# Two attention blocks on a batch of eight: where a stage's weight sums, one job's statistics and one layer's output bias are made

## The chip, the core and the metric

The kernel runs on one core of a Trainium2 chip, in one launch. The metric is the time of one execution on the device in microseconds (us); less is better. All arithmetic is in float32.

## What is computed

The input x has 8 images of 512 channels and 32 x 32 positions. Two layers of the same kind are applied to each image. A layer normalises x over 8 groups of channels, makes q, k and v by products with 512 x 512 weights, runs attention with 8 heads of 64 channels over the 1024 positions, multiplies by an output weight and adds x. The second layer has the same form with weights of its own.

```python
xg = x.reshape(B, GROUPS, -1)
xn = ((xg - mean) * lax.rsqrt(var + EPS)).reshape(B, C, H, W) * gamma + beta
qkv = einsum('oc,bchw->bohw', qkv_w, xn) + qkv_b
attn = softmax(einsum('bhds,bhdt->bhst', q, k) * scale, axis=-1)
out = einsum('bhst,bhdt->bhds', attn, v).reshape(B, C, H, W)
return x + einsum('oc,bchw->bohw', proj_w, out) + proj_b
```

## The kernel before

A **job** is one image in one layer. There are 16, in the order (image 0, layer 0), (1, 0), (0, 1), (1, 1), (2, 0), (3, 0), (2, 1), ... (L103). The jobs are numbered from 0, so job 2 is the first of layer 1 and job 3 the fourth of all. For every job the kernel runs two sections, which follow each other on TensorE without overlap:

- **Stage n** makes what attention n needs and finishes what attention n-1 left: first v of job n (`v_phase`, L482), then in `deep_phases` (L574) the output product O of job n-1 and k and q of job n. In this text "stage 2" is the one with O of job 1 and k and q of job 2.
- **Attention n** (`Attention.run`, L984) has 64 steps: four score products (L870), ScalarE's exp (L875), VectorE's running sum of the exponentials (L885, L887), and four value products two steps later (L901). After every eight steps `finish` closes a group (L917 to L978). Chores, small jobs of the next stage, are hung on step numbers (slots).

**The products of a stage.** All four weights are multiplied by a seven-product scheme (Strassen's, in Winograd's form). For O, k and q it is nested: seven outer **chains**, and in each chain seven products of 128 x 128 by 256 columns. So `deep_phases` has 21 chains c = 0 to 20: 0 to 6 are O, 7 to 13 k, 14 to 20 q. The seven products of a chain run in the order 1, 5, 6, 2, 7, 3, 4 and two chains are interleaved (L762): the product at place j of chain c stands at 7c + 2j. ScalarE copies or adds a bias (L438, L442, L646, L648, L657). VectorE reads PSUM after product 7 and after product 3 (L653, L655, in `put`). Product 4 adds to the bank that VectorE has to read after product 7, so TensorE can't start product 4 before that read has ended.

**What VectorE does between the reads.** After product 7 and after product 3 of a chain there is a **slot** (L744): it takes one thing from the first of three queues that is not empty: `soon`, `outer`, `extra`. `soon` holds sums that the coming chains need. `outer` holds the additions that put the outer products together (L668), among them the additions of O's parts to x (L684). `extra` holds work of later sections, each with the chain before which it isn't taken: the statistics of the job after (L234), the loading of an output bias and its four sums (`make_out_bias`, L1065). What `extra` still holds at the end of the stage is put on the first slots of the attention that follows (L1298).

**Weight sums.** A chain needs seven 128 x 128 matrices: four come from DRAM, and three are their sums, made in place with four VectorE instructions (`prepare`, L194, through `factor`, L151). It is done the first time a weight is used, and the result is stored in DRAM for all later jobs. So layer 0's O is prepared in stage 1, layer 1's k and q (14 chains) in stage 2 and layer 1's O in stage 3. `begin(c)` (L586), which runs with the first product of chain c, prepares chain c + 2. VectorE's order is the program's, so those four instructions stand ahead of whatever VectorE instruction comes next, which is the read after product 7 of chain c - 1.

**Additions to x by DMA.** Some of O's parts are added to x not by VectorE but by an accumulating DMA that GpSimd issues (L682, in `more`, L674). In stage 2 there are four: parts 1 and 2 to the quarter (0, 0) of x, part 3 to the quarter (0, 1), part 4 to the quarter (1, 0). VectorE adds the other parts to the same quarters. The framework keeps accesses to the same bytes in the order in which the program issues them, by semaphores. Each outer product lies in a buffer of a pool of six (`epool`), which the exponentials of the attention use as well.

**Statistics.** `norm_steps(n)` (L355) gives the steps of job n's normalisation. Usual form: eight `bn_stats` on VectorE in `extra`, a gather over DRAM (L271), then in the attention before job n the group values (L281), the factors (L301) and four ScalarE passes that write the normalised x (L308). Job 1 has another form: in attention 0 ScalarE makes the sums and the sums of squares (`sums` L242, `squares` L251) in eight passes over x, whose main output goes to the buffer of the normalised x and is overwritten later. With that form the chores have later slots (L1301 to L1304), and the additions on the normalised x (L377 to L391 in `combine`) stand at slots 41, 44, 47, 50 and not at 36, 39, 42, 45.

The engines TensorE, VectorE and ScalarE run in the program's order (`manual_schedule`, L1544). The framework orders the queues of SyncE and GpSimd, so a load can be issued ahead of where the program has it, once its buffer is free.

Of the kernel before, what the change touches and what calls it, by code (L numbers as in the profile page):

```python
# [28 lines left out]
NT = S // P  # L29
HALF = S // 2  # L30
HP = NH // 2
NVEC = 6 * NC
GAMMA, BETA, BQ, BK, BP, BV = (i * NC for i in range(6))
SUM_LIMIT = 1e10
# [38 lines left out]
def fast_path(  # L73
# [281 lines left out]
    def norm_steps(n):  # L355
        norm = Norm(n)

        def place():
            xn[0] = acts.tile([P, NC, S], F32, tag="xn", name=f"xn_{n}")

        def factors():
            norm.factors(slice(0, NC))
            if n > 1:
                place()

        if n == 1:
            reads = [place] + [lambda cc=cc: norm.sums(cc) for cc in range(NC)]
            reads.append(norm.less_mean)
            reads += [lambda cc=cc: norm.squares(cc) for cc in range(NC)]
            reads.append(lambda: (norm.by_count(), norm.gather()))  # L370
            return reads, [norm.groups, factors] + [lambda cc=cc: norm.apply(cc) for cc in range(NC)]
        reads = [lambda cc=cc, sh=sh: norm.stat(cc, sh) for cc in range(NC) for sh in range(2)]
        reads.append(norm.gather)
        steps = [norm.groups, factors] + [lambda cc=cc: norm.apply(cc) for cc in range(NC)]
        return reads, steps
# [198 lines left out]
    def deep_phases(n, extra, outs=None, early=()):  # L574
# [8 lines left out]
        def job(which):  # L583
            return n - 1 if which == O else n

        def begin(c):  # L586
            which, o = chains[c]
            m = job(which)
            b, layer = jobs[m]
            if o == OUTER[0] and which != O:  # L590
                name = "k" if which == K else "q"
                dst[which] = acts.tile([P, NC, S], F32, tag=name, name=f"{name}_{n}")
                (kt if which == K else qt)[0] = dst[which]
            if c + 2 < len(chains):
                ahead, oo = chains[c + 2]
                prepare((job(ahead), ahead, oo))
            if which == O and c in (3, 4):
                soon.extend(outs.steps(c + 2))
            e = epool.tile([P, 2, HALF], F32, tag="e", name=f"p_{n}_{c}")
            tiles[which, o] = e  # L600
            s5 = small.tile([P, QT], F32, tag="s5", name=f"s5_{n}_{c}", bufs=3)
            half = (c + len(chains)) % 2
            ends = c + 1 == len(chains)
            names = "yvzu" if ends else ("vyuz", "zyuv")[(c // 2) % 2]
            z, y, u, w = (bank(half, b, f"{b}d_{n}_{c}")[:, :QT] for b in names)
            if which == O:
                r = right(outs.src, to[0], o)
                sums = outs.at[c]
            else:
                r = right(xn[0], tx[0], o)  # L610
                if o in (4, 5, 6):
                    d = deep_t[0][:, :, {5: 0, 6: 1, 4: 2}[o], :]
                else:
                    d = deep_x[0][:, :, {1: 0, 7: 1, 2: 2, 3: 3}[o], :]
                sums = [d[:, i, :] for i in range(4)]
            moving = {
                1: r[:, 0, :QT], 2: r[:, 1, :QT], 3: r[:, 1, QT:],
                5: sums[0], 6: sums[1], 7: sums[2], 4: sums[3],
            }
            lhs = held[m, which, o]  # L620

            def bias(oo):
                if o in (1, 6, 7):
                    return None
                oc = oo if o == 2 else 2 + oo
                if which == O:
                    return (
                        out_step[:, layer, oo : oo + 1] if o == 3
                        else out_bias[:, layer, oc : oc + 1]
                    )  # L630
                if o == 3:
                    return bias_step[:, layer, int(which == Q), oo : oo + 1]
                return env.vec(layer, BK if which == K else BQ, oc)

            def product(i, ps, start):
                nc.tensor.matmul(  # L636
                    ps, lhs[:, FACTOR[i], :], moving[i], start=start, stop=True,
                    skip_group_check=True,
                )

            def put(oo, ph, ps):
                to_ = e[:, oo, ph * QT : (ph + 1) * QT]
                b = bias(oo)
                if ph == 0:
                    if b is None:
                        nc.scalar.copy(to_, ps)  # L646
                    else:
                        nc.scalar.activation(to_, ps, AF.Identity, bias=b)  # L648
                elif ends and oo == 1:
                    nc.scalar.activation(to_, ps, AF.Identity, bias=b)  # L650
                    nc.vector.tensor_add(to_, to_, s5)
                elif b is None:
                    nc.vector.tensor_add(to_, ps, s5)  # L653
                else:
                    nc.vector.scalar_tensor_tensor(to_, ps, b, s5, ALU.add, ALU.add)  # L655

            return chain(product, lambda ps: nc.scalar.copy(s5, ps), put, z, y, u, w)  # L657
# [618 lines left out]
    for n in range(-1, len(jobs)):  # L1276
        last = n + 1 == len(jobs)
        outs = None
        if n >= 0:
            chores = {}  # L1280

            def put(i, fn):
                while i in chores:
                    i += 1
                chores[i] = fn

            if last:
                w = last_weights(n)
                for i, fn in enumerate(last_sums(0)):
                    put(44 + 3 * i, fn)  # L1290
            else:
                if n == 0:
                    first_factors(put, [(O, 0), (V, 1)])
                elif n == 1:
                    first_factors(put, [(K, 1), (Q, 1)])
                elif n == 2:
                    first_factors(put, [(O, 1)])
                for i, (_, fn) in enumerate(extra):  # L1298
                    put(2 + i, fn)
                at = (10, 19, 22, 24, 26, 28, 36, 39, 42, 45)  # L1300
                if n == 0:  # L1301
                    for i, fn in zip((3, 3, 4, 5, 6, 8, 10, 11, 12, 13, 15), reads):
                        put(i, fn)
                    at = (22, 30, 34, 35, 37, 38, 41, 44, 47, 50)  # L1304
                for i, fn in zip(at, steps + sums(n + 1)):
                    put(i, fn)
                deep_first = deep_steps(n + 1)
                for at, fn in zip((52, 54, 57, 59), deep_first[4:]):
                    put(at, fn)
                put(61, lambda: (extend_plan(n + 1), [fetch() for _ in range(RING)]))  # L1310
            assert max(chores, default=0) < NT * len(att.groups)
            att.run(chores)
            banks(0, "one")
            banks(1, "one")
            if last:
                for i, fn in enumerate(last_sums(1)):
                    later(4.1 + 1.5 * i, fn)
                later(9.9, judge)
                for sh in range(2):
                    last_proj(n, w, sh)  # L1320
                break
            outs = OutputSums(n)
            out_sums(n, outs)
            first = v_phase(n + 1, ORDER)
            for thunk in first[:-1]:
                thunk()
            rest = first[-1:]
            extra = deque()
            if jobs[n][1] == 1 and jobs[n][0] + 2 < B:
                extra.append((11, lambda b=jobs[n][0] + 2: (x_tile(b), load_x(b))))  # L1330
            if n == 1:
                load, bias_steps = make_out_bias(1)
                extra.append((8, load))
                extra.extend((11, fn) for fn in bias_steps)
            if n + 2 < len(jobs):
                reads, steps = norm_steps(n + 2)
                extra.extend((15, fn) for fn in reads)
        both = deep_phases(n + 1, extra, outs, deep_first[:4] if outs else ())
        both[0]()
        rest[0]()  # L1340
        if n < 0:
            later(22.0, lambda: load_x(1))
        for thunk in both[1:]:
            thunk()
        banks(0, "two")
        att = Attention(n + 1)
        att.scores(0)
        att.scores(1)
        banks(1, "two")
        att.scores(2, "po")  # L1350
# [249 lines left out]
```

## Time and profile before

| what | value |
|---|---|
| runs of the kernel before | 3206.60, 3208.58 and 3208.76 us, median 3208.58 us |
| the profiled execution's own time | 3205.31 us |
| span of its profile | 3203.5 us |
| TensorE busy | 3184.0 us, 99% |
| VectorE busy | 2773.0 us, 87% |
| ScalarE busy | 1913.1 us, 60% |
| GpSimd busy | 100.7 us, 3% |
| chain that ended last | TensorE 95%, VectorE 4% |
| bytes moved | 308.32 MB, 96 GB/s over the span |

The span runs from the first to the last instruction; 1.8 us of the execution's time lie around it. In the views below, a line names an instruction by its line in the kernel, its engine, its operation and what it writes and reads ("out<-in", buffer numbers left out). PE is TensorE's matmul, PEld its weight load, DVE VectorE, ACT ScalarE, POOL GpSimd. In a list of waits the engine and instruction that waited stand left of the arrow and the one that let it go right of it, with the total in us, the number of times and the longest. In a timeline each line has the start and the duration in us, and in brackets how long the engine was idle before it and who released it. Matmuls are pipelined and their ends are modelled, so a short wait of TensorE shows a little smaller than it is.

### The profile page before, as it was taken

What the parts mean: (1) busy time and instruction counts of PE and PEld (TensorE: products, weight loads), DVE (VectorE), ACT (ScalarE), POOL (GpSimd) and SP (SyncE); (2) the same over time, 40 slices, a digit from 0 to 9 for tenths busy, and PEclk for the clock granted to TensorE, in tenths of its full rate; (3) what the DMA queues carried; (4) which work ended last, traced back from release to release, by engine and by line L of the source; (5) the groups of instructions that cost most, each with busy time, mean ns of one, the idle gap of its engine ahead of it and who ended that gap; (6) DMA issues with size and microseconds to landing.
All of it is one profiled execution on the core that took longest, in us unless ns stands there. A gap on an engine that the chain in (4) does not pass through costs nothing.

```text
span 3203.5 us, 57787 instructions
## 1 busy us (share of the span) xinstructions
PE 3184.0 (99%) x22917; PEld 1861.8 (58%) x22917; DVE 2773.0 (87%) x3989; ACT 1913.1 (60%) x3063; POOL 100.7 (3%) x95
## 2 busy tenths in 40 slices
PE   9999999999999999999999999999999999999999
PEld 7366384663836648366483754837547375573844
DVE  8897999979889798897988889888898888988877
ACT  4746646466565665656656565565656656566564
POOL 0000000000000000000000000000000000000000
PEclk9999999999999999999999999999999999999999
DMA  8234172350703315033160421505216051150511
GB/s 291 74 108 126 49 215 69 94 167 22 213 25 91 88 28 159 21 105 130 30 210 16 119 67 38 147 16 142 96 44 194 16 141 44 51 135 20 170 37 42
DMA packets 156998, 308.32 MB, mean 96 GB/s; under 512 B 34104, under 2 KB 60592, under 8 KB 156464
## 3 DMA queue, kind: packets, MB, share of 16 engines
q1 hardware_dynamic: 139856, 272.05, 26.5%
q0 software_dynamic: 16864, 32.51, 6.2%
q8 instruction: 181, 2.97, 0.4%
q14 instruction: 97, 0.79, 0.1%
HBM read 225.13 MB, written 45.68 MB: 85 GB/s over the span
## 4 chain that ended last, share of the span: by engine, by line
PE 95%; DVE 4%; DMA 0%; issue 0%; POOL 0%; ACT 0%; DVEq 0%; POOLq 0%
PE sc L870 27%; PE po L901 27%; PE zd L636 10%; PE vd L636 10%; PE z L494 6%; PE yd L636 5%; PE ud L636 4%; PE y L494 2%; PE v L494 2%; PE u L494 2%; DVE acc L887 0%; DMA x<-p 0%; PE z_last L814 0%; DVE w L156 0%; DVE p L655 0%
## 5 line engine op out<-in xcount | busy, mean ns | idle before, releaser
L875 ACT ACTIVATE e<-sc 128x1024 f32<-128x1024 f32 x1024 | 1044.3, 1024 | 564.2 <-PE sc L870 458.7
L870 PE MATMUL sc<-q,k 64*64 64x512 f32 x8192 | 1058.2, 589 | 0.0
L901 PE MATMUL po<-e,v 64*64 64x512 f32 x8192 | 1057.3, 589 | 0.0
L887 DVE TENSOR_TENSOR acc<-acc,e 128x1024 f32<-128x1024 f32 x768 | 936.4, 1219 | 58.7 <-ACT e L875 12.0
L901 PEld LDWEIGHTS po<-e,v 64*64 64x64 f32 x8192 | 313.2, 133 | 565.7 <-issue 553.3
L870 PEld LDWEIGHTS sc<-q,k 64*64 64x64 f32 x8192 | 311.5, 133 | 562.4 <-issue 544.8
L885 DVE TENSOR_TENSOR acc<-e,e 128x1024 f32<-128x1024 f32 x128 | 156.4, 1222 | 112.2 <-ACT e L875 112.1
L636 PE MATMUL zd<-deep,w 128*128 128x256 f32 x860 | 241.1, 380 | 2.7 <-DVE p L653 2.1
L636 PE MATMUL vd<-deep,w 128*128 128x256 f32 x804 | 224.3, 380 | 1.4 <-DVE p L655 1.3
L636 PEld LDWEIGHTS zd<-deep,w 128*128 128x128 f32 x860 | 162.8, 190 | 27.2 <-DVE p L653 3.4
L636 PEld LDWEIGHTS vd<-deep,w 128*128 128x128 f32 x804 | 152.3, 190 | 23.9 <-DVE p L655 2.5
L917 DVE TRANSPOSE_TENSOR_REDUCE r<-acc 128x32 f32<-128x1024 f32 x128 | 158.5, 1238 | 0.6
L682 POOL DMA_DIRECT2D x<-p x62 | 74.6, 1211 | 1971.4 <-ACT p L646 1525.1
L636 PE MATMUL vd<-os,w 128*128 128x256 f32 x420 | 118.1, 380 | 1.6 <-DVE p L655 1.6
L668 DVE TENSOR_TENSOR p<-p,p 128x1024 f32<-128x1024 f32 x94 | 114.2, 1215 | 0.0
L494 PE MATMUL z<-w,t 128*128 128x256 f32 x480 | 110.9, 379 | 0.0
L494 PE MATMUL z<-w,xn 128*128 128x256 f32 x480 | 110.1, 382 | 0.0
L518 ACT COPY v<-z 128x512 f32<-128x512 f32 x32 | 18.7, 585 | 148.7 <-PE z L494 148.7
L494 PEld LDWEIGHTS z<-w,xn 128*128 128x128 f32 x480 | 90.0, 190 | 23.8 <-issue 12.2
L442 ACT COPY ud<-zd 128x256 f32<-128x256 f32 x156 | 55.7, 357 | 76.6 <-PE zd L636 75.7
L653 DVE TENSOR_TENSOR p<-vd,s 128x256 f32<-128x256 f32 x63 | 26.7, 424 | 85.1 <-PE vd L636 85.1
L657 ACT COPY s<-vd 128x256 f32<-128x256 f32 x156 | 58.0, 372 | 69.7 <-PE vd L636 69.7
(242 smaller groups left out, 4192.6 us busy)
## 6 DMA issues: line engine op xcount, KB each, us to landing
w<-deep SPq DMA_DIRECT2D x287, 448.0 KB, 3.8
x<-p POOLq DMA_DIRECT2D x62, 512.0 KB, 6.6
rb<-rd SPq DMA_DIRECT2D x96, 256.0 KB, 4.0
w<-keep SPq DMA_DIRECT2D x84, 256.0 KB, 2.7
deep<-w SPq DMA_DIRECT2D x42, 448.0 KB, 3.7
w<-wqkv_dram SPq DMA_DIRECT2D x57, 256.0 KB, 2.8
x<-x_dram SPq DMA_DIRECT2D x28, 512.0 KB, 6.4
out_dram<-x SPq DMA_DIRECT2D x28, 512.0 KB, 6.4
```

What stands on the lines that cost most here:

```text
L442: nc.scalar.copy(u, z)
L494: nc.tensor.matmul(ps[:, ti * CH : (ti + 1) * CH], right(src, tx[0], o)[:, cc, t0 : t0 + P], w[:, cc, :], start=(start and ti == 0 and cc ...
L636: nc.tensor.matmul(ps, lhs[:, FACTOR[i], :], moving[i], start=start, stop=True, skip_group_check=True,)
L657: return chain(product, lambda ps: nc.scalar.copy(s5, ps), put, z, y, u, w)
L668: outer.append(lambda: nc.vector.tensor_add(to_, a, b))
L682: nc.gpsimd.dma_start(to_, p(part), accum_op=ALU.add)
L870: nc.tensor.matmul(sc[h * HD : (h + 1) * HD, j, :], k[r, hp, k0 : k0 + HD], q[r, hp, sh * HALF : (sh + 1) * HALF], start=True, stop=True,)
L875: nc.scalar.activation(e, sc, AF.Exp, scale=SCALE)
L885: nc.vector.tensor_add(acc[g], self.es[i - 1], e)
L887: nc.vector.tensor_add(acc[g], acc[g], e)
L901: nc.tensor.matmul(po[g][j * HD : (j + 1) * HD, h, :], v[r, kc, d0 : d0 + HD], e[r, j, :], start=(kc == 0), stop=(kc == NT - 1),)
L917: nc.vector.tensor_reduce(self.r[:, 0, m, :], self.acc.pop(g).rearrange("p j (b e) -> p (j b) e", e=RP), AX.X, ALU.add, apply_transpose=True,)
```

## The change

There are three edits:

1. Job 3 gets job 1's form of statistics: a constant `ALONE = (1, 3)` takes the place of the tests for job 1 alone. Its eight `bn_stats` leave stage 2 and the first slots of attention 2. ScalarE makes the sums in attention 2, and that attention's chores take the later slots.
2. Layer 1's output bias is loaded and summed in stage 1 and not in stage 2: the load from chain 9 on (it was 8), the four sums from chain 12 on (it was 11). They stand ahead of job 2's statistics in the queue `extra`.
3. In `begin(c)` a weight of k or q that has yet to be prepared, for a job after the first, is prepared not at once but by an entry in the queue `soon`, so that it runs in a slot, after a read of PSUM. That concerns the 14 chains of stage 2 and no other stage. `soon` goes ahead of `outer`, so the entries of `outer` come later than before.

```diff
+ALONE = (1, 3)
...
         def factors():
             norm.factors(slice(0, NC))
-            if n > 1:
+            if n not in ALONE:
                 place()
 
-        if n == 1:
+        if n in ALONE:
             reads = [place] + [lambda cc=cc: norm.sums(cc) for cc in range(NC)]
...
             if c + 2 < len(chains):
                 ahead, oo = chains[c + 2]
-                prepare((job(ahead), ahead, oo))
+                key = (job(ahead), ahead, oo)
+                if key in raw and n > 0 and ahead != O:
+                    soon.append(lambda: prepare(key))
+                else:
+                    prepare(key)
             if which == O and c in (3, 4):
...
                 at = (10, 19, 22, 24, 26, 28, 36, 39, 42, 45)
-                if n == 0:
+                if n + 1 in ALONE:
                     for i, fn in zip((3, 3, 4, 5, 6, 8, 10, 11, 12, 13, 15), reads):
                         put(i, fn)
                     at = (22, 30, 34, 35, 37, 38, 41, 44, 47, 50)
...
-            if n == 1:
+            if n == 0:
                 load, bias_steps = make_out_bias(1)
-                extra.append((8, load))
-                extra.extend((11, fn) for fn in bias_steps)
+                extra.append((9, load))
+                extra.extend((12, fn) for fn in bias_steps)
             if n + 2 < len(jobs):
                 reads, steps = norm_steps(n + 2)
-                extra.extend((15, fn) for fn in reads)
+                if n + 2 not in ALONE:
+                    extra.extend((15, fn) for fn in reads)
```

## The prediction, made before the changed kernel ran

> **What bounds the kernel now.** I read first the page's busy times and its chain, then one table of windows with five stages, then the waits of TensorE in stage 2, then timelines.
>
> ```profile
> PE 3184.0 (99%) x22917; PEld 1861.8 (58%) x22917; DVE 2773.0 (87%) x3989; ACT 1913.1 (60%) x3063; POOL 100.7 (3%) x95
> ...
> PE 95%; DVE 4%; DMA 0%; issue 0%; POOL 0%; ACT 0%; DVEq 0%; POOLq 0%
> ```
>
> TensorE sets the time; only its holes can be won. The windows show where they lie: stages 1, 2, 3, 4 and 6.
>
> ```profile
> core 0: us, PE busy (x) PEld busy (x) DVE busy (x) ACT busy (x) POOL busy (x), PEclk, DMA share, GB/s
> 191.80:285.60 93.80, 89.76 (x414) 76.33 (x410) 78.87 (x152) 46.54 (x116) 6.18 (x5) 1.00 0.57 166
> 395.60:488.30 92.70, 89.97 (x414) 76.39 (x410) 86.07 (x189) 46.48 (x116) 4.80 (x4) 1.00 0.65 196
> 598.30:688.00 89.70, 88.44 (x410) 76.65 (x406) 76.73 (x150) 46.56 (x116) 6.00 (x5) 1.00 0.71 220
> 798.00:885.90 87.90, 87.90 (x414) 77.05 (x410) 71.87 (x123) 46.55 (x116) 4.80 (x4) 1.00 0.66 198
> 1193.70:1281.60 87.90, 87.90 (x414) 77.04 (x410) 71.92 (x123) 46.55 (x116) 4.80 (x4) 1.00 0.56 151
> ```
>
> A stage without holes lasts 87.9 us. Stage 1 is 5.9 longer, stage 2 4.8, stage 3 1.8. The change touches stage 2 above all, so 4.8 us (0.15% of the time) is nearly all that it can win. In stage 2 TensorE waits only for VectorE's reads of PSUM:
>
> ```profile
> PE vd L636 <- DVE p L655: 1.2, 3, 0.6
> PE zd L636 <- DVE p L655: 0.7, 1, 0.7
> PE zd L636 <- DVE p L653: 0.6, 1, 0.6
> ```
>
> VectorE's timeline there shows why: the four sums of a weight stand straight ahead of the read (L655).
>
> ```profile
> 437.86 0.28 DVE L154 TENSOR_TENSOR w<-w 128x128 f32<-128x128 f32 x1
> 438.18 0.29 DVE L156 TENSOR_TENSOR w<-w 128x128 f32<-128x128 f32 x1
> ...
> 438.59 0.28 DVE L160 TENSOR_TENSOR w<-w 128x128 f32<-128x128 f32 x1
> 438.79 0.48 DVE L655 SCALAR_TENSOR_TENSOR p<-vd,out_step,s 128x256 f32<-128x256 f32 x1
> 439.19 1.22 DVE L684 TENSOR_TENSOR x<-x,p 128x1024 f32<-128x1024 f32 x1
> ```
>
> From start to start: weight sums 0.93 us, a read 0.33 (L653) or 0.40 (L655), an addition of 1024 columns 1.13.
>
> [...] the accumulating moves (L682) take 5.7 to 10.5 us. [...] the trace shows such a wait in stage 1:
>
> ```profile
> 242.51 0.48 DVE L655 SCALAR_TENSOR_TENSOR p<-ud,out_bias,s 128x256 f32<-128x256 f32 x1
> 245.35 1.23 DVE L684 TENSOR_TENSOR x<-x,p 128x1024 f32<-128x1024 f32 x1 [2.37 <-DMA x<-p]
> 246.49 0.42 DVE L653 TENSOR_TENSOR p<-zd,s 128x256 f32<-128x256 f32 x1
> ```
>
> There TensorE waited 1.5 us as shown, some 1.6 in truth, for the read at 246.49. So 2.37 us of VectorE's wait cost TensorE about 0.75 less than itself.
>
> **Part 1: the weight sums go behind the reads (stage 2).** Nothing is removed: 14 x 0.93 = 13.0 us on VectorE as before. In a chain's period VectorE now has two reads (0.66 to 0.80), the sums (0.93) and one addition (1.13): 2.72 to 2.86 us. TensorE's period is seven products at 0.431 us from start to start in stage 6: 3.02. So the reads come on time, and stage 2's 4.8 us go. What is late next is the additions: before, both slots of a chain took them, now one does. In the changed program's order VectorE has, after chain 4's reads: sums, `p6+p1`; chain 5: sums, x(0,1) += part 6; chain 6: sums, x(0,1) += part 5. The DMA that adds part 3 to that same quarter is issued at the end of chain 5, which is now between those two additions; before, both stood ahead of it. So the addition after chain 6 **waits for this DMA to land**, with VectorE's queue, the next reads among it, behind it.
>
> Its price, from VectorE's starts. Chain 4's first read 434.93; +0.33 and +0.93 to its second read, +0.33 to the addition, +1.13 = 437.7, chain 5's first read; +0.40 +0.93 +0.40 +1.13 = 440.5, end of the addition that the DMA waits for. GpSimd issues some 0.4 later, 440.9. Landing L later. In stage 6 the third move takes 5.7 us, in stage 2 6.7 beside the bias's 1.25 MB, which goes, and the stores of weights, which stay:
>
> ```profile
> DMA to landing us min/median/max: 5.7/7.0/7.0
> ```
>
> (moves of stage 6). I take L = 6.1: 447.0. VectorE comes to the addition at 440.8 (chain 6's first read, as TensorE delivers it in stage 6, moved to stage 2) + 0.40 + 0.93 + 0.40 = 442.5. It waits 4.5 us, TensorE 4.5 - 0.75 = 3.8. After that 2.86 of 3.02 us lets VectorE catch up; the later additions are a few tenths late for ScalarE's next use of a buffer, which its idle time covers. Stage 2: -4.8 + 3.8 = **-1.0 us**. The bounds: [...] L = 10.5 (stage 1's longest move) gives 8.2[...]. [...]
>
> What else hangs on the weight sums: they run one product after `begin(c)`, 13 products (5.6 us) ahead of chain c + 2, so even the 4.5 us wait leaves them in time. Their stores (448 KB, SyncE) are issued about 1 us later, and the fetches behind them in SyncE's queue are for chains some seven periods (21 us) off: 0. On GpSimd's queue the fourth move follows the third; it now has no addition of VectorE ahead of it, and its landing, some 3 us after the third's, is needed only near 454 us: 0.
>
> **Part 2: layer 1's bias in stage 1.** Four sums at 0.68 us and two small instructions go into slots that were empty or had statistics; in stage 1 VectorE waits over 1 us in each of these chains, so 0. In stage 2 the four sums (2.7 us) and four statistics (2.7) leave VectorE; that is what makes one free slot a chain, and it is counted in part 1. The load is 1.25 MB through SyncE's queue; its order has it between the fetches of k's weights, from about 227 us on, and the DMA engines are full from 220 to 252 us. The move that VectorE waits for at 245.35 can land later; each us is one of TensorE's. The bias made stage 2's third move about 0.9 us slower than stage 6's: I take **+0.6**, from 0[...] to +1.5. The weights fetched behind the load come 2 to 3 us later, and are needed some seven chains (21 us) on: 0. Two statistics of job 2 go over to attention 1, so its gather starts some 3.7 us later and VectorE may wait up to 2 us for it ahead of L286. The next exponentials' sums are queued behind it; the ring of six exponentials, whose next user is some 6 us off, hides this. Without that cover it would cost at most 2.
>
> **Part 3: ScalarE's sums for job 3.** In attention 2: 4 x (1.06 + 0.20) + 4 x (1.14 + 0.19) = 10.4 us, from attention 0's rows, against 35.5 us that ScalarE idles ahead of the exponentials there. Attention 0 does the same and lasts 110.1 us, the others 110.0: **+0.1**. The later slots also move two additions (2.3 us) past slot 41. Attention 0 has this: its last L924 starts 5.8 us after the attention's end (197.58), in attention 2 3.4 (601.68), and TensorE waited 1.1 us for it. In attention 2 VectorE will be less behind at slot 41, by 0.3 to 0.85 us, since job 1's v weights are not summed there. So stage 3 begins with a wait of 0.25 to 0.8: **+0.5**, bounds 0 (it had no wait there) and 1.1 (attention 0's).
>
> **The sum.** -1.0 + 0.6 + 0.1 + 0.5 = +0.2 us on the profiled execution's 3205.31 (span 3203.5 and 1.8 around it): 3205.5. The median of the runs is 3.3 above that execution: **3208.8**. In terms of L: change = L - 5.9.
>
> **The rivals.**
> - *The DMA is no wait*: [...] the additions are further behind than I have them. Stage 2 loses all or most of its 4.8 us; with +1.2 elsewhere -2.7 to -3.6: about 3205.4. For it: [...] the change does take 1.25 MB out of this stage. Against: no move in the trace took under 5.7.
> - *The DMA is a long wait*: L near 10 us, as in stage 1; then +4.1, 3212.7. It turns to a loss from L = 5.9. For it: stage 2's DMA engines have raw weights to fetch and sums to store besides. Against: the same move took 6.7 with even more beside it.
> - *The weight sums don't leave the path*: VectorE's reads stay late in all chains for some reason, stage 2 keeps its 4.8 us and gets the wait as well: +5 or more, 3213.6. Against: 2.86 of 3.02.
>
> **How the numbers follow.** Forecast 0.60 (L from 5 to 7.5: 3207.7 to 3210.2), no wait 0.20, long wait 0.14, the last 0.06. The range is 3205.0 to 3212.0: it leaves out most of the last case and the end of the long wait. About 0.2% (6.4 us) is what a measurement of this kernel can tell from no change. No case reaches it on the fast side, since 4.8 us is all that there is; the slow side takes a long wait with other losses. Faster 0.02, same 0.94, slower 0.04.
>
> **What would show it.** In the changed profile: stage 2 at about 91.7 us; in VectorE's timeline a wait of some 4.5 us for the DMA x<-p ahead of an L684 instruction near 443 us, and TensorE's waits for L653 and L655 otherwise gone; stage 1 at 94 to 95; attention 2 at 110.1; a wait of TensorE for L924 at the start of stage 3. No such wait for the DMA, or a stage 2 under 89 us, would show my central step wrong.

## The result, and the profile after

The changed kernel takes 3211.66 us (median of 22 runs, 3210.25 to 3213.04), and the kernel before, on the same chip, 3207.03 us (22 runs): ratio 1.0014, interval 1.0008 to 1.0020. It is 4.6 us slower; 3208.8 had been forecast. (The 3208.58 us given earlier for the kernel before is the median of the first three of these 22 runs.) The profiled execution has a span of 3211.1 us.

```profile
PE 3186.8 (99%) x22916; PEld 1865.0 (58%) x22917; DVE 2768.0 (86%) x3979; ACT 1921.7 (60%) x3079; POOL 100.7 (3%) x95
...
PE 93%; DVE 6%; issue 1%; DMA 1%; ACT 0%; SPq 0%; POOL 0%; DVEq 0%; POOLq 0%
```

VectorE has 5 us less to do, ScalarE 8.6 more, and TensorE is the bound as before. In the chain that ended last VectorE has 6% and not 4%, and DMA, which had nothing, 1%. Lines of the code after L597 carry a number higher by 5: the read L653 is L658, L655 is L660, the addition L684 is L689, the product L636 is L641, the move L682 is L687, L924 is L929. This is the table of windows of the changed kernel (busy us and number of instructions of each engine, TensorE's granted clock, DMA share, GB/s), with stages 1, 2, 3, 4 and 6:

```profile
193.10:288.60 95.50, 89.71 (x410) 76.29 (x406) 80.47 (x159) 46.58 (x116) 6.18 (x5) 1.00 0.60 177
398.60:494.60 96.00, 91.18 (x414) 78.58 (x410) 80.38 (x172) 45.98 (x116) 4.80 (x4) 0.96 0.62 176
604.60:695.50 90.90, 89.26 (x414) 76.54 (x410) 78.21 (x151) 46.70 (x116) 6.00 (x5) 1.00 0.70 218
805.50:893.40 87.90, 87.90 (x414) 77.08 (x414) 72.09 (x124) 46.59 (x116) 4.80 (x4) 1.00 0.66 198
1201.20:1289.10 87.90, 87.90 (x414) 77.07 (x413) 71.85 (x124) 46.60 (x116) 4.80 (x4) 1.00 0.56 151
```

Taken to two digits from TensorE's timeline (first product of a stage to the first score product after it), the three stages went from 93.81, 92.65 and 89.72 us to 95.55, 95.94 and 90.87: +1.74, +3.29, +1.15. Attention 2 stayed at 110.03. That is 6.2 us. Stage 0 was 1.3 longer too: there the clock stayed at one half for 6.8 and not 3.4 us at the very start. That is not the change's doing, since the second profile of the kernel before (e7) has 6.8 as well. The profiled execution of before was faster than all its 22 runs (3205.31; they go from 3205.87 to 3211.2) and that of the changed kernel one of its slowest (3212.94), so the medians differ by less than the profiles.

Stage 2 is where the surprise lies: its clock column says 0.96. The five small waits of TensorE are gone, and one long wait stands in their place:

```profile
PE zd L641 <- DVE p L658: 4.8, 1, 4.8
```

VectorE's timeline of the changed kernel shows why (start, duration, in brackets the idle time and who ended it):

```profile
442.54 1.21 DVE L689 TENSOR_TENSOR x<-x,p 128x1024 f32<-128x1024 f32 x1
...
445.16 0.48 DVE L660 SCALAR_TENSOR_TENSOR p<-ud,out_bias,s 128x256 f32<-128x256 f32 x1
451.32 1.23 DVE L689 TENSOR_TENSOR x<-x,p 128x1024 f32<-128x1024 f32 x1 [5.68 <-DMA x<-p]
452.46 0.42 DVE L658 TENSOR_TENSOR p<-zd,s 128x256 f32<-128x256 f32 x1
```

The addition of part 6 to the quarter (0, 1) of x ends at 443.7, GpSimd issues the accumulating move of part 3 to the same quarter, and VectorE comes to the addition of part 5 at 445.6 and has to wait 5.68 us for that move. GpSimd's timeline has the third and the fourth move:

```profile
444.29 1.20 POOL L687 DMA_DIRECT2D x<-p  x1 [8.97 <-ACT yd L439]
446.33 1.20 POOL L687 DMA_DIRECT2D x<-p  x1 [0.84 <-ACT p L653]
```

The third landed at 451.30. The time from its issue to its landing, L in the prediction, is 7.0 us. What ran beside it shows in the DMA queues: q0 carries GpSimd's moves and q1 SyncE's transfers. These are the packets, the MB and the share of the 16 engines' time (packets overlap) in the 2.77 us from the third move's first packet on, above in the changed kernel and below in the run e5, where L is 5.0:

```profile
q0 software_dynamic: 145, 0.30, 62.4%
q1 hardware_dynamic: 128, 0.46, 45.0%
...
q0 software_dynamic: 256, 0.52, 110.5%
q1 hardware_dynamic: 1, 0.00, 0.3%
```

A move is 256 packets of 2 KB. In e5 all of them go out in this time; in the changed kernel 145 do, and the 128 packets of a store of weight sums (448 KB) go out between them. SyncE issued this store 0.98 us after the move, and 1.55 us after it in e5 and in before. The fourth move is not in the way: its first packet goes out at 451.25, when the third's last (450.69) is gone. And then TensorE's timeline:

```profile
447.52 0.59 PE L641 MATMUL vd<-deep,w 128*128 128x256 f32 x2
452.93 1.22 PE L641 MATMUL zd<-deep,w 128*128 128x256 f32 x2 [4.82 <-DVE p L658]
453.94 1.06 PE L641 MATMUL yd<-xn,w 128*128 128x256 f32 x2
454.80 1.06 PE L641 MATMUL vd<-t,w 128*128 128x256 f32 x2
...
459.22 0.59 PE L641 MATMUL yd<-t,w 128*128 128x256 f32 x2
```

A product stands in the trace as two instructions. Ahead of the wait a product takes 0.43 us from start to start; after it 0.86, up to 458.2. The clock column of the same stretches:

```profile
452.90:458.50 5.60, 5.57 (x13) 4.49 (x14) 3.76 (x12) 1.58 (x4) 0.00 (x0) 0.50 0.57 164
458.50:462.00 3.50, 3.50 (x17) 3.08 (x17) 2.83 (x8) 1.89 (x5) 0.00 (x0) 1.00 0.41 104
```

For 5.6 us TensorE looks fully busy and does half its work. Against a stage without holes (87.83 us), TensorE lost 5.1 us by the wait (5.20 from instruction to instruction, less the 0.22 that it takes anyway, plus the 0.10 by which the instruction after a wait is late at full clock too, as in stage 1 of before), another 2.7 at the half clock (13 instructions, each 0.14 to 0.27 us late), and 0.3 in small delays further on: 8.1 us.

### The profile page after: what moved, and what is told of

It is laid out like the page before. It is cut to its first block, busy times and chain, and to the rows that moved or that the text cites. A ratio compares the mean times of both kernels' runs of the same rounds, so it can differ in the third digit from the quotient of the medians.

```text
span 3211.1 us, 57801 instructions
## 1 busy us (share of the span) xinstructions
PE 3186.8 (99%) x22916; PEld 1865.0 (58%) x22917; DVE 2768.0 (86%) x3979; ACT 1921.7 (60%) x3079; POOL 100.7 (3%) x95
## 4 chain that ended last, share of the span: by engine, by line
PE 93%; DVE 6%; issue 1%; DMA 1%; ACT 0%; SPq 0%; POOL 0%; DVEq 0%; POOLq 0%
PE sc L875 26%; PE po L906 26%; PE zd L641 10%; PE vd L641 10%; PE z L495 6%; PE yd L641 5%; PE ud L641 4%; DVE acc L892 2%; PE u L495 2%; PE y L495 2%; PE v L495 1%; DMA x<-p 1%; DVE q L983 0%; PE z_last L819 0%; DVE acc L890 0%
## 5 line engine op out<-in xcount | busy, mean ns | idle before, releaser
L641 PE MATMUL zd<-deep,w 128*128 128x256 f32 x860 | 241.9, 381 | 8.1 <-DVE p L658 6.2
L641 PE MATMUL vd<-deep,w 128*128 128x256 f32 x804 | 224.6, 380 | 0.5 <-DVE p L660 0.4
L641 PEld LDWEIGHTS zd<-deep,w 128*128 128x128 f32 x860 | 163.3, 191 | 32.5 <-DVE p L658 7.0
L641 PEld LDWEIGHTS vd<-deep,w 128*128 128x128 f32 x804 | 153.0, 191 | 22.6 <-DVE p L660 0.8
L687 POOL DMA_DIRECT2D x<-p x62 | 74.6, 1211 | 1944.1 <-ACT p L651 1523.3
L641 PE MATMUL vd<-os,w 128*128 128x256 f32 x420 | 118.3, 380 | 1.4 <-DVE p L660 1.3
L658 DVE TENSOR_TENSOR p<-vd,s 128x256 f32<-128x256 f32 x63 | 26.7, 424 | 85.9 <-PE vd L641 85.8
```

The lines of the kernel that those rows point to most:

```text
L641: nc.tensor.matmul(ps, lhs[:, FACTOR[i], :], moving[i], start=start, stop=True, skip_group_check=True,)
L687: nc.gpsimd.dma_start(to_, p(part), accum_op=ALU.add)
```

## The experiments

Theory A: edit 3 costs stage 2 a wait for the third move **and** the half clock after it; edit 2 wins about 2 us there and loses them in stage 1; edit 1 costs stage 3. Rivals: the late weight sums do harm elsewhere in stage 2 (B), or stages 1 and 3 differ only by chance from one execution to the next (C). Each run's stage lengths, from its own trace (the medians are from several chips; the kernel before, run beside each, had 3206.67 to 3207.14 us there):

| kernel | stage 1 | stage 2 | attention 2 | stage 3 | 2nd move of stage 1, us to landing | 3rd move of stage 2 | median us |
|---|---|---|---|---|---|---|---|
| before | 93.8 | 92.7 | 110.0 | 89.7 | 6.8 | 6.7 | 3207.03 |
| before, second profile | 94.8 | 92.6 | 110.0 | 94.7 | 7.5 | 7.4 | one run |
| changed | 95.6 | 95.9 | 110.0 | 90.9 | 8.3 | 7.0 | 3211.66 |
| e1 no edit 3 | 96.6 | 90.8 | 110.0 | 91.8 | 8.5 | 5.0 | 3207.54 |
| e2 edit 2 alone | 96.4 | 90.8 | 110.0 | 89.7 | 8.3 | 5.0 | one run |
| e3 filled wait | 95.6 | 93.5 | 110.0 | 91.2 | 8.5 | 7.2 | 3210.41 |
| e4 edit 1 alone | 96.1 | 91.9 | 110.0 | 91.2 | 8.0 | 7.4 | one run |
| e5 late slots | 96.1 | 89.3 | 110.0 | 91.4 | 8.5 | 5.0 | 3205.25 |
| e6 bias in attention 2 | 95.0 | 95.7 | 110.0 | 93.0 | 7.5 | 7.0 | one run |
| b1 | 95.1 | 89.3 | 118.8 | 90.8 | 7.6 | 5.0 | 3211.87 |
| b2 | 95.8 | 89.4 | 110.0 | 89.9 | 8.6 | 5.0 | 3204.43 |
| b3 | 94.2 | 89.4 | 114.5 | 89.7 | 7.6 | 5.0 | 3207.56 |
| g2 | 94.1 | 87.8 | 114.3 | 91.4 | 6.8 | 5.6 | 3206.33 |
| g3 | 94.9 | 87.8 | 111.7 | 91.1 | 7.5 | 5.6 | 3206.28 |

**Without edit 3** (e1): every weight is prepared at once again.

```diff
-                if key in raw and n > 0 and ahead != O:
-                    soon.append(lambda: prepare(key))
-                else:
-                    prepare(key)
+                prepare(key)
```

> The changed kernel with one edit undone: the weight sums of k and q are again made at once in begin(c), the statistics on ScalarE and the early bias stay. My theory (stage 2's loss is the addition to x that waits for the accumulating DMA, followed by a stretch of TensorE at half rate): no wait for a DMA in stage 2; the first three waits of the kernel before stay (2.4 us), its later ones go with the bias and the statistics, so stage 2 lasts 90 to 91 us against 95.9. Stages 1 and 3 stay at 95.5 and 90.9. Whole: about 5 us faster than the changed kernel, 0 to 1 us slower than the kernel before. Rival (the bias and the late chores cost the time, the weight sums are a gain): stage 2 near the 92.6 of before and the whole 2 us or less from the changed kernel.

Measured: 3207.54 us, ratio to before 1.0000 (0.9991 to 1.0008). So edits 1 and 2 together show no change of the time, and the loss of 0.14% is edit 3's. Stage 2 goes from 95.9 to 90.8, as expected; stages 1 and 3 came out 1.0 and 0.9 us longer than in the changed kernel, which was not.

**The bias alone** (e2): before, with only the load and its sums moved a stage sooner.

```diff
-            if n == 1:
+            if n == 0:
                 load, bias_steps = make_out_bias(1)
-                extra.append((8, load))
-                extra.extend((11, fn) for fn in bias_steps)
+                extra.append((9, load))
+                extra.extend((12, fn) for fn in bias_steps)
```

> The kernel before with the bias edit alone: layer 1's output bias in stage 1. Theory (the 1.25 MB load makes the accumulating moves of stage 1 land later): stage 1 at 95 to 95.6 us against 93.8, with a new wait for an x<-p move near 50 us into the stage; stage 2 at 91.5 to 92.3 against 92.65, since four sums leave it; stage 3 unchanged at 89.7. Rival (stage 1's loss is not the load but a difference between executions): stage 1 at 93.8.

Measured: one run, 3205.78 us. Stage 2 gains 1.9 us, more than expected, and stage 3 is as before. Stage 1 is 96.4, longer than expected: TensorE waits 3.1 us there, from instruction to instruction, for ScalarE's copy L438, and the clock falls to 0.50 for 3.4 us.

**The wait filled** (e3): the changed kernel, with eleven products whose results nobody uses, put into TensorE's queue right ahead of the product that waits. Nothing else differs.

```diff
+FILL = 11
...
-            return chain(product, lambda ps: nc.scalar.copy(s5, ps), put, z, y, u, w)
+            step = chain(product, lambda ps: nc.scalar.copy(s5, ps), put, z, y, u, w)
+
+            def filled(i):
+                if i == 4 and n == 2 and c == 7:
+                    for _ in range(FILL):
+                        nc.tensor.matmul(
+                            w, lhs[:, FACTOR[1], :], moving[1], start=True, stop=True,
+                            skip_group_check=True,
+                        )
+                step(i)
+
+            return filled
```

> The changed kernel with 11 more products of TensorE (0.431 us each, 4.7 us in all; their results are not used) in front of product 4 of chain 7 in stage 2, where TensorE stands still for some 5 us. Theory (the half rate after that wait comes from TensorE having been idle): the filled wait costs nothing, no half rate follows, stage 2 at 93.3 us against 95.9, the whole 2.6 us faster than the changed kernel. Rival (the half rate is due to late data or to busy DMA engines, not to the idle time): the half rate stays, stage 2 at 95.9 or longer.

Measured: 3210.41 us, ratio 1.0010 (1.0003 to 1.0017). VectorE's line has the same wait, and somewhat longer; TensorE's windows have no drop of the clock:

```profile
450.94 1.23 DVE L701 TENSOR_TENSOR x<-x,p 128x1024 f32<-128x1024 f32 x1 [5.91 <-DMA x<-p]
```

```profile
447.00:452.60 5.60, 5.30 (x26) 4.33 (x24) 1.66 (x3) 0.41 (x2) 0.00 (x0) 1.00 1.09 220
452.60:458.50 5.90, 5.90 (x28) 5.22 (x29) 5.80 (x16) 3.47 (x9) 0.00 (x0) 1.00 0.76 224
```

In the 5.9 us after the wait TensorE starts 28 instructions, against 13 in 5.6 us of the changed kernel, and stage 2 is 2.5 us shorter (93.5). So the half clock is a cost of its own, on top of the wait, and it comes from TensorE's idle time: VectorE was no less late, and the DMA engines were no less busy after the wait (0.76 against 0.57). The times alone don't tell the two kernels apart, since their intervals overlap; the traces do.

**Edit 1 alone** (e4): before, with `ALONE = (1, 3)` and what hangs on it, and neither of the other edits.

```diff
+ALONE = (1, 3)
...
-                if n == 0:
+                if n + 1 in ALONE:
```

> The kernel before with the statistics edit alone: job 3's sums by ScalarE in attention 2 and that attention's later slots. Theory: stage 3 at 90.7 to 90.9 us against 89.7, with a wait of TensorE for L924's successor at its start; attention 2 at 110.0 to 110.1; stage 2 between 91 and 92.6, since four statistics leave its slots; stage 1 at 93.8. Rival (stage 3's loss in the changed kernel was handed on from stage 2): stage 3 at 89.7.

Measured: one run, 3207.88 us; stage 2 91.9 (0.7 less), stage 3 91.2 (1.5 more). Stage 1 is 96.1 though its program issues the same work as before's, no bias among it. There ScalarE waited for the second move, TensorE 2.2 us for ScalarE, and the clock fell here too; ScalarE's line and TensorE's window:

```profile
243.29 0.47 ACT L650 ACTIVATE p<-yd,out_bias 128x256 f32<-128x256 f32 x1 [3.01 <-DMA x<-p]
```

```profile
244.09:248.00 3.91, 3.91 (x10) 3.17 (x11) 2.19 (x3) 1.81 (x5) 1.20 (x1) 0.56 1.08 253
```

So rival C has something: stage 1 is not the same from one execution to the next. The next three runs ask about that.

**Late slots** (e5): the changed kernel, with the first three k weights (chains 7 to 9) prepared at once and the other eleven in slots, so that all of VectorE's additions to x are issued ahead of the moves.

```diff
-                if key in raw and n > 0 and ahead != O:
+                if key in raw and n > 0 and ahead != O and c >= 8:
```

> The changed kernel, but in stage 2 the weight sums of the first three k chains (chains 7, 8 and 9) are made at once again and stand ahead of the reads; those of the other eleven stay in slots. So all of VectorE's additions to x are issued ahead of the moves again. Theory A (the wait for the third move, and TensorE's lower clock after it, are the whole loss of edit 3): stage 2 falls from 95.9 us to 90.2 to 90.5, the three waits of 0.3, 0.7 and 0.6 us for a read at the chains 7 to 9 being all that is left over 87.8; the time falls by 5 to 5.7 us to some 3206 to 3207. Rival B (weight sums in slots cost stage 2 elsewhere too, by late additions or late stores): stage 2 stays at 92 or more and the time falls by under 4 us.

Measured: 3205.25 us, ratio to before 0.9995 (0.9986 to 1.0003), 6.4 us less than the changed kernel (6.1 by the two ratios). TensorE's waits in its stage 2 are these, and VectorE waits for no DMA there:

```profile
PE zd L641 <- DVE p L660: 0.7, 1, 0.7
PE vd L641 <- DVE p L660: 0.3, 1, 0.3
```

Stage 2 lasts 89.3, even a little less than expected. Theory A holds and B falls: with the additions ahead of the moves, weight sums in slots do what they were meant to. L is 5.0 here as well, but with the additions ahead nothing waits for it.

**The bias in attention 2** (e6): loaded into a half of a buffer that is free there, and summed at four slots; the lines of edit 2 are taken out, so that neither stage has it. (How the load takes a part of that buffer is left out here.)

```diff
-                    first_factors(put, [(O, 1)])
+                    load, bias_steps = make_out_bias(1)
+                    first_factors(put, [(O, 1)], load)
+                    for i, fn in zip((17, 19, 20, 24), bias_steps):
+                        put(i, fn)
```

> The changed kernel, but layer 1's bias is loaded and summed in attention 2 (into a buffer that is free there), so neither in stage 1 nor in stage 2. Theory A (the 1.25 MB load made stage 1's moves late): stage 1 goes from 95.5 us back to 93.8. Rival B (stage 1's moves land early or late from one execution to the next, load or no load, as the run with edit 1 alone suggests with 96.1 us): stage 1 is anywhere from 93.8 to 96.5, and the second move of stage 1 lands 7 to 8.5 us after its issue though no bias is fetched. Stage 2 as in the changed kernel, 93.4 to 95.9 us. The additions in attention 2 stay under VectorE's idle time: 110.0 us.

Measured: one run, 3212.42 us. Stage 1 lasts 95.0 and its second move takes 7.5 us: nearer to the rival, though that move lands sooner than in any run with the bias in stage 1. Stage 2 repeats the changed kernel's (95.7): a wait of 4.8 us, L = 7.0, and the half clock (0.50 from 452 to 456 us).

**Before, once more** (e7), unchanged.

> The kernel before, unchanged, for a second profile of it. Theory A (stage 1's 93.8 us belong to its program): 93.8 again, stages 2 and 3 at 92.7 and 89.7, second move of stage 1 in 6.8 us. Rival B (stage 1 varies from one execution to the next): stage 1 at 95 us or more, its second move in about 8 us, with the same program.

Measured: 3212.06 us in the profiled run. Stage 1 lasts 94.8 with the same program. And stage 3 is 5.0 us longer than in the first profile, by a wait for a weight:

```profile
PE vd L636 <- DMA w<-deep: 3.1, 1, 3.1
```

after which the clock fell again (0.57 on average from 680 to 684 us). One trace for each kernel is too few for stages 1 and 3. Over all traces, the second move of stage 1 lands in 8.3 to 8.6 us where the bias is fetched in stage 1 (six traces: changed, e1, e2, e3, e5, b2) and in 6.8 to 8.0 where it isn't (the eight others); stage 1 lasts 96.0 against 94.8 us on average. The bias costs stage 1 about 1.2 us, and the rest of the difference of 1.74 is that the first trace of before is the shortest of its eight. The lengths overlap, so the 1.2 is a mean and not a bound.

**Three parts together** (b1): e5's condition, e6's bias, and attention 2's chores back at slots not far from the usual ones.

```diff
+                    if n == 2:
+                        at = (21, 27, 28, 30, 31, 33, 36, 39, 42, 45)
```

> Weight sums in slots only from the fourth k chain on, layer 1's bias in attention 2, job 3's statistics on ScalarE but with attention 2's chores at their usual slots. Theory: stage 1 as before, 93.8 to 96 us; stage 2 90.2 to 90.5; stage 3 89.7, since the additions on the normalised x come early again; so 2.2 to 2.5 us less than before, about 3204.8. Rival: the chores at their usual slots meet ScalarE's sums in attention 2 and make it longer than 110.1 us, or stage 3 waits as in the changed kernel (90.9); then 3206 or more.

Measured: 3211.87 us, ratio 1.0013 (1.0006 to 1.0019). The rival. Stage 2 is 89.3, but attention 2 lasts 118.8. ScalarE's and VectorE's timelines:

```profile
543.05 1.24 ACT L312 ACTIVATE xn<-x,off,mul 128x1024 f32<-128x1024 f32 x1 [6.75 <-DVE off L307]
```

```profile
542.46 0.16 DVE L305 TENSOR_TENSOR mul<-mr,vec_sb 128x4 f32<-128x4 f32 x1 [1.32 <-DMA mr<-dg]
```

ScalarE stands at the pass that writes the normalised x, the next exponentials are queued behind it, TensorE waits 5.7 us and then runs at half clock (0.52 on average from 544 to 548 us). e6 has the same bias and ScalarE's sums with the late slots, and its attention 2 lasts 110.0: with both, the group values come too late for the pass at the earlier slots. Which of the two makes them late isn't separated here; the bias's sums do a part of it, as b3 shows.

**Edit 1 undone** (b2): e5, with the statistics left on VectorE as before.

```diff
-ALONE = (1, 3)
+ALONE = (1,)
```

> The changed kernel with the weight sums in slots from the fourth k chain on, and with edit 1 undone: job 3's statistics stay eight bn_stats on VectorE and attention 2 keeps its usual slots; layer 1's bias in stage 1 as in the change. Theory (edit 1 only costs: it makes stage 3 wait for late chores, and stage 2's slots have room for the statistics once the bias has left): stage 1 94 to 96.5 us, stage 2 89.3 to 89.8, attention 2 110.0, stage 3 89.7 in place of 90.9 to 91.4. So 1.2 to 1.6 us less than the run with late slots alone: 3203.8, some 3.3 us less than before. Rival (the statistics need the slots that the weight sums now take): stage 2 at 90.5 or more, or a wait in attention 2, and 3205 or more.

Measured: 3204.43 us, ratio 0.9992 (0.9983 to 1.0000); 2.2 us less than before. Its windows for stages 1, 2 and 3:

```profile
193.20:289.00 95.80, 89.76 (x410) 76.43 (x406) 80.13 (x159) 46.55 (x116) 6.18 (x5) 1.00 0.60 176
399.10:488.40 89.30, 88.31 (x410) 76.84 (x406) 81.54 (x174) 46.47 (x116) 4.80 (x4) 1.00 0.66 189
598.40:688.30 89.90, 88.62 (x410) 76.68 (x406) 76.78 (x150) 46.55 (x116) 6.00 (x5) 1.00 0.71 220
```

Stage 3 is back, and the statistics cost TensorE nothing in stage 2 or attention 2. This is the lowest median of the study, though its interval ends at no difference and overlaps with those of e5, g2 and g3.

**The bias in attention 2 without edit 1** (b3): b2 with e6's bias.

```diff
-            if n == 0:
-                load, bias_steps = make_out_bias(1)
-                extra.append((9, load))
-                extra.extend((12, fn) for fn in bias_steps)
...
+                    first_factors(put, [(O, 1)], load)
+                    for i, fn in zip((17, 19, 20, 24), bias_steps):
+                        put(i, fn)
```

> As the kernel with edit 1 undone, and layer 1's bias is loaded and summed in attention 2 and not in stage 1. Theory (the bias's load costs stage 1 about 1 us on average, by later moves): stage 1 93.8 to 95.1 us, stages 2 and 3 as there, so some 1 us less: 3202.8. Rival (stage 1's length is chance): no difference, 3203.8.

Measured: 3207.56 us, ratio 1.0002 (0.9994 to 1.0011). Stage 1 is 94.2, but attention 2 is 114.5: the bias's sums took slots of that attention, and the chores behind them moved on by some slots. ScalarE waits again ahead of the same pass:

```profile
533.54 1.24 ACT L312 ACTIVATE xn<-x,off,mul 128x1024 f32<-128x1024 f32 x1 [3.02 <-DVE off L307]
```

**GpSimd makes the first three sums** (g2): b3, with the three weights that still stood ahead of reads summed by GpSimd. (`prepare` hands its second argument on to `factor`, which is left out here.)

```diff
-                    prepare(key)
+                    prepare(key, nc.gpsimd if n == 2 and ahead == K else None)
```

> As the kernel with the bias in attention 2, but the sums of the first three k weights of stage 2, which still stand ahead of reads, are made by GpSimd. Theory (VectorE's queue is what makes the reads late, whoever else makes the sums is free): stage 2's waits of 0.3 and 0.7 us go, stage 2 at 87.9 to 88.6 in place of 89.3. Rival (GpSimd is slow: its one small arithmetic instruction in the trace, 8x1, takes 1.43 us, so four sums take 5.7 us or more, about as long as the 5.6 us until the chain needs them, and the moves are queued behind them): TensorE waits for the weights or for later moves, stage 2 at 90 to 95 us.

Measured: 3206.33 us, ratio 0.9997 (0.9989 to 1.0006). Stage 2 has no wait of TensorE left (87.8). GpSimd's timeline, third weight:

```profile
435.22 0.64 POOL L156 TENSOR_TENSOR w<-w 128x128 f32<-128x128 f32 x1
435.93 1.45 POOL L158 TENSOR_TENSOR w<-w 128x128 f32<-128x128 f32 x1
437.35 1.50 POOL L160 TENSOR_TENSOR w<-w 128x128 f32<-128x128 f32 x1
438.81 0.45 POOL L162 TENSOR_TENSOR w<-w 128x128 f32<-128x128 f32 x1
```

Twelve such sums take 9.8 us, 0.82 each against VectorE's 0.28. They end ahead of the third move (issued at 441.64) and in time for their chains; the rival had judged by another instruction, of 1.43 us, which was too unlike these. Attention 2 keeps b3's loss (114.3).

**The bias under VectorE's wait** (g3): g2, with the bias's sums at slots 7, 8, 9 and 11.

```diff
-                    for i, fn in zip((17, 19, 20, 24), bias_steps):
+                    for i, fn in zip((7, 8, 9, 11), bias_steps):
```

> As the kernel whose first three k weights of stage 2 are summed by GpSimd, but the bias's four sums stand at slots 7, 8, 9 and 11 of attention 2 and not at 17, 19, 20 and 24. There VectorE waited 3.3 us for the gather ahead of slot 10, which covers most of their 2.7 us, and the chores of slots 19 to 28 keep their places. Theory (the 4.3 us of attention 2 came from the pushed chores alone): attention 2 back at 110.0 us, stage 1 93.8 to 95.1, stage 2 87.8, stage 3 89.7; in all some 3201.7 to 3202.3 us, 5 less than before. Rival (VectorE has no room for the bias in attention 2, wherever it stands): attention 2 at 111 or more, or stage 3 at 91 or more, and 3203.5 or more.

Measured: 3206.28 us, ratio 0.9997 (0.9989 to 1.0006). The times are the rival's, though not for its reason alone: two of job 3's left-over statistics were pushed behind the bias's sums, the gather came later, VectorE waited 4.7 us for it, attention 2 lasts 111.7 and stage 3 91.1. What wasn't tried is g2's GpSimd sums on b2, with the bias in stage 1.

## Why the prediction was right, and where its sum was not

The time fell into the range, and the wait that was named is there. Its size was not right: stage 2 was forecast 1.0 us shorter and came out 3.3 longer. That 3211.66 lies inside 3205.0 to 3212.0, by 0.3 us, was partly luck: the range was wide, the time is above the 3207.7 to 3210.2 of the forecast's own case, and in the profiled executions the three stages alone add 6.2 us, where the range had room for 3.4. A sum of +0.2 us has no sign that a measurement could confirm.

- **Reads on time, -4.8 us.** Right: of all the waits of stage 2 only the one for the move is left.
- **VectorE comes to the addition at 442.5, the move is issued at 440.9.** Stage 2 starts 3.0 us later in the changed trace; taken off, they are 442.6 and 441.3. Right to 0.4.
- **L = 6.1.** It was 7.0. The term that failed is the one on the stores of the weight sums: "issued about 1 us later ... 0". It asked only when the fetches behind the stores are needed, and not what a store does beside the third move. Measured from the stage's start, the move is issued at 45.7 us in both kernels. The first of these stores is indeed 1.1 us later than before, but the third, the one behind the move, is at 46.6 and not at 47.3, so sooner, and it goes out in the middle of the move. It does so in all three traces where the store follows 0.98 us after the move (changed, e3, e6), and L is 7.0, 7.2 and 7.0. In e1, e2, e5, b1, b2 and b3 it follows 1.55 us after the move, its packets start as the move's last ones go out, and L is 5.0 each time. (In g2 and g3 no store but a weight's fetch is issued 1.64 us after it, and L is 5.6.) With the bias fetched in stage 2, L is 6.7, 7.4 and 7.4 (before, e7, e4). So taking the bias away was worth about 2 us of L (e2 against before), and the earlier store gave them back. That is shown by the packets of these traces; a kernel that holds this store back alone was not run. "0" for the fourth move was right: it landed 3.0 us after the third, and TensorE didn't wait for it. "No move in the trace took under 5.7" was misread: stage 2's own first move took 5.4, the shortest of the 62 in the first trace of before. A move short enough to leave no wait (under 1.6 us, by the sum's own 440.9 and 442.5) was not shown.
- **TensorE loses 3.8.** VectorE waited 5.68 us in place of 4.5 (0.4 from the issue, 0.9 from L), and TensorE lost 5.1, which is 0.6 less. Counted in the same way, stage 1 of before gives 0.6 too, where the sum took 0.75: that step held.
- **Nothing about the clock.** The sum has no term for it, and it cost 2.7 us, the largest single error. I had forecast 3.8 us of idle time for TensorE and priced its length alone. In these traces no wait of up to 2.2 us, measured from instruction to instruction, lowered the clock to 0.50, and ten of the eleven from 2.5 us on did (one each in changed, e1, e2, e4, e5, e6, e7, b1, b3 and g2; b2's 2.8 did not). What goes with it shows in the traces' own clock records. In each of the fourteen traces all changes of the clock lie whole multiples of 3.413 us apart (to 0.01 us in before and changed). Cut the traces into windows at these points (without the first 20 and the last 15 us): ten windows at full clock have TensorE busy for 1.26 us or less, and the clock is 0.50 after each of them; no other has under 1.47 us, and it stays at 1.00. So in these traces it is TensorE's work in one such window that goes with the half clock, and a window with up to 1.26 us of work in it was followed by it too. b2's wait of 2.83 us was cut in two by the end of a window; most of e5's wait of 2.86 fell into one. Here are e5's window and the next, then b2's two, with the columns of the tables above:

```profile
242.59:246.00 3.41, 0.93 (x5) 0.79 (x5) 1.65 (x3) 1.18 (x4) 0.00 (x0) 1.00 1.08 255
246.00:249.41 3.41, 3.41 (x10) 2.66 (x9) 1.41 (x2) 1.43 (x4) 1.20 (x1) 0.50 1.10 285
...
240.09:243.50 3.41, 2.89 (x14) 2.21 (x12) 2.19 (x3) 0.83 (x2) 1.20 (x1) 1.00 1.07 246
243.50:246.91 3.41, 1.47 (x7) 1.32 (x8) 2.01 (x3) 1.71 (x5) 0.00 (x0) 1.00 1.06 279
```

  The changed kernel's wait left one window without any work and ran 1.3 us into the next. So the clock fell at 451.66, before the wait was over, and stayed low for two windows.
- **Stage 1, +0.6 (0 to 1.5).** +1.74 in these two traces, outside the bounds; about 1.2 over all traces, inside them, and by the way that was named, a move that lands late behind the bias. The move is the second and not the one that VectorE waited for, and ScalarE waits as well.
- **Attention 2, +0.1.** Right: 0.0. The other cost that was named, chores at wrong places, shows in b1 and b3.
- **Stage 3, +0.5 (0 to 1.1).** +1.15. The wait for L929 at the start came, and cost 0.56 us (0.29 shown). The term missed that VectorE stays behind: two instructions further on were late by 0.24 and 0.34 more. e3 and e4 have 1.5.

The rival with the long wait (L near 10, 3212.7) came nearer in time than the forecast, but by another way: L was only 0.9 longer than I took it, which by the sum's own formula makes +1.1 and not +0.2. In the profiles the half clock (2.7) and stages 1 and 3 (1.8 more than forecast) weigh more.

## What to carry to other kernels

When an edit moves the issue of a DMA, ask which other transfer it now runs beside, and not only when its data is needed: here a store let go 0.6 us sooner went out in the middle of a move, the move landed 2 us later, and that was the one somebody waited for. Put VectorE's accesses to a buffer all ahead of an accumulating DMA to it in the order of the program; that (e5 against the changed kernel) was worth some 6 us. All behind it with room may do as well, which was not run. And price a long wait of TensorE at more than its length, or fill it: ten of the eleven waits of 2.5 us or more were followed by the half clock, which took 2.7 us besides in the changed kernel and some 1.6 in e4.

## What the runs showed that was not expected

- In each of the fourteen traces all changes of the clock lie whole multiples of 3.413 us apart. Ten windows of that length in which TensorE was busy for 1.26 us or less were followed by the half clock, none with 1.47 us or more was (from 20 us after the start to 15 us before the end). So two waits of the same length can differ in price: 2.8 us cost the clock in e5 and not in b2.
- The clock stood at 0.50 for 6.8 us with waits of 5.2 us (changed, e6), and for 3.4 us with waits of 2.5 to 3.1 (e1, e2, e4, e5).
- A move of 512 KB landed 7.0 to 7.2 us after its issue in the three traces where a store of 448 KB went out among its packets, and 5.0 in the six where the store went out behind them.
- Eleven products without use in the wait kept the clock at 1.00.
- GpSimd made a float32 sum of 128x128 in 0.82 us on average, 0.44 to 1.50, that is 2.9 times VectorE's 0.28.
- The same program differs by up to 5 us in one stage between two executions (stage 3 of before: 89.7 and 94.7), by when a fetched weight lands.
